# The order of 32-row and 64-row score products in a cross-attention kernel

## The chip, the cores and the metric

The kernel runs on one core of one Trainium2 chip. The metric is the device time of one execution in microseconds (us), the median of several runs. Five engines work from queues of their own: TensorE (PE in the profile, its weight loads PEld), VectorE (DVE), ScalarE (ACT), GpSimd (POOL) and SyncE (SP), which issues most of the DMAs. TensorE reads SBUF and writes PSUM; the results leave PSUM through VectorE and ScalarE.

## The reference

An image cross-attention layer on 16 items (the batch), float32, one after the other: 100 query rows of 640 numbers, 718 context rows of 384 numbers and 4 extra tokens of 384 numbers each. There are 8 heads of 80 numbers.

```python
query = hidden_states @ Wq            # (16, 100, 640)
keyt  = enc @ Wk                      # (16, 718, 640)
valt  = enc @ Wv
hs    = _mha(query, keyt, valt)       # softmax(q k^T / sqrt(80)) v, 8 heads
ca_q1 = einsum('btc,th->bch', ca, Wq_ca)[:, indices, :]   # 100 of 384 rows
ca_hs1 = _mha(ca_q1, residual, residual)                  # residual = hidden_states
ca_hs2 = _mha(ca_hs1 @ Wq, ca @ Wk_ca, ca @ Wv_ca)        # 4 tokens
out   = (hs + ca_hs2) @ Wout + b_out + residual
```

## The kernel before

**Stages.** One loop runs over the 16 items (`for b in range(B)`, called item 0 to item 15 here). Its order is written out by hand: the program stands in a manual schedule, so each engine executes its instructions in the order of the source. For item b the loop makes the scores of the 718 keys (`scores`, three groups), the larger of all scores per query (`larger`, then a `Maximum`, which spreads one maximum over 32-wide blocks: transposes and reductions on VectorE, two `spread` copies, on ScalarE where `scalar` is set), subtracts it, takes exponentials, and multiplies by the values (`a_ps`, line 1806). Beside that it makes the values of item b (`Values`, `vv`) and the keys of item b+1 (`Keys`, `kk`, and `Chunk` for the last 128 columns). Both use sums of the inputs' blocks to save products: `enc_sums` makes 13 such sums of 128x240 numbers on Pool for each item, of the context of item b+2, while item b runs.

The second attention (the 4 tokens, class `Second`) runs in small pieces between: `products` makes `y_ps` on TensorE out of `m2`, which `keys` fills on Pool from m's columns (`load_m` brings them from DRAM by a DMA on SyncE's queue); `copy` takes `y_ps` out (ScalarE to `y_sb`, line 968, and VectorE to `g`, line 964); `scores1` multiplies the tokens out on Pool (lines 980, 987); `softmax1` and `exponentials1` follow on VectorE and ScalarE; `softmax2` makes `z_ps` on TensorE; `scores2` subtracts a maximum (line 1062, on VectorE in item 1, on Pool in items after it); `values2` makes the result `hs2` on Pool from pieces `vb`, which SyncE loads, two ahead. `seen` is the last instruction of `larger(2)`; some loads and the first product of `scores1` are held back behind it.

Items are treated in three kinds: `MIXED` (3, 5, 7, 9, 11, 13), `PLAIN` (2, 4, 10, 12, 14) and the rest.

**Scores.** The 718 keys are cut into three thirds and each third into two halves of 120 or 119 keys; `KC` lists the six. A group g of `scores` covers two of them and fills four PSUM banks: bank r holds heads 2r and 2r+1. A head has 80 numbers; 64 of them stand in `qp`, two heads on top of each other in 128 partitions, the other 16 of each head stand in a common block `qz`, two heads in 32 rows. So there are 64-row products (`first_rows`: 64 partitions by 64 or 56 columns, four tiles of the array at once) and 32-row products (`last_rows`: 32 partitions by 120 columns, four at once). Each shows as two records in the profile (float32). A group has 64 records of the former and 16 of the latter.

```python
def first_rows(last):
    for a in range(2):
        u, j = KC[2 * g + a]
        for c in range(RG):        # 4 pairs of heads: c and 4 + c
            ...
...
steps = (last_rows, first_rows) if g == 1 else (first_rows, last_rows)
for i, step in enumerate(steps):
    step(i == 1)
```

Groups 0 and 2 take two pairs of banks (pool `ps2`), group 1 takes two banks of pool `psk` and two of pool `ps1`. The pools have two buffers of each kind. Just before item b's scores, `psk` holds the two banks of the last item's `a_ps` (head groups g = 0 and 1), and `ps1` holds that item's last key products and `y_ps`; `z_ps`, made behind the scores, is of `ps1` too. ScalarE copies the scores to SBUF (`st`): two copies of two banks each in groups 0 and 2 (line 837), four of one bank each in group 1 (line 831).

**The end of an item.** TensorE makes `a_ps` of head group 0, then of head group 1, with the steps of `Chunk` and of `softmax1` between them. `read(g)` divides by the sum of the exponentials and adds `hs2`: a reciprocal and four VectorE instructions (lines 1749, 1764). In PLAIN items both reads stand behind the last product; item 14 alone reads head group 0 earlier, with four ScalarE instructions and an addition on Pool (line 1773). Then come `products` and `copy` for item b+2's second attention, and item b+1's scores.

Of the kernel before, what the change touches and what calls it, by code (L numbers as in the profile page):

```python
# [14 lines left out]
B, S, H = 16, 100, 640  # L15
NH, D = 8, 80
CAD, T = 384, 4
SK = 722 - T
P = 128
HC = H // P  # L20
# [99 lines left out]
def kernel(  # L120
# [354 lines left out]
                at[:, : 2 * KT].rearrange("p (i k) -> p i k", i=2),  # L475
            )

    def enc_sums(enc):

        at = lambda f: a_form(enc, f)  # L480
        raw = lambda u, c: a_raw(enc, u - 1, c - 1)
        for out, left, right, op in (
            (at(7), raw(2, 3), raw(3, 1), ALU.add),
            (at(11), raw(3, 2), raw(3, 3), ALU.add),
            (at(8), at(11), raw(2, 3), ALU.subtract),
            (at(10), raw(1, 3), at(11), ALU.subtract),
            (at(9), raw(2, 1), raw(2, 2), ALU.add),
            (at(2), raw(1, 1), at(9), ALU.subtract),
            (at(9), at(9), raw(3, 1), ALU.subtract),
            (at(5), raw(1, 1), raw(2, 1), ALU.subtract),  # L490
            (at(5), at(5), raw(2, 3), ALU.add),
            (at(11), raw(1, 3), raw(3, 3), ALU.subtract),
            (at(11), at(11), raw(3, 1), ALU.add),
            (at(4), at(2), at(10), ALU.add),
            (at(4), at(4), raw(1, 2), ALU.add),
        ):
            nc.gpsimd.tensor_tensor(out, left, right, op)  # L497

    def w4(c, g):
# [266 lines left out]
    def scores(b, g, tiles):  # L766

        qp, qz = tiles
        name = f"s_ps_{b}_{g}"
        if g == 1:  # L770
            s_ps = [f(f"{name}_{r}") for r, f in enumerate((psumk, psumk, psum1, psum1))]
        else:
            pairs = [pair(f"{name}_{i}") for i in range(2)]
            s_ps = [pairs[r // 2][:, r % 2] for r in range(RG)]
        n = KN
        begun = set()

        def product(at, part, w, rhs, cols, last):

            k0, k1 = part  # L780
            nc.tensor.matmul(  # L781
                s_ps[at][k0:k1, cols],
                w,
                rhs,
                start=not begun & {(at, k) for k in range(k0, k1, 32)},
                stop=last,
                skip_group_check=True,
            )
            begun.update((at, k) for k in range(k0, k1, 32))

        def first_rows(last):

            for a in range(2):
                u, j = KC[2 * g + a]
                for c in range(RG):
                    rhs = qp[:, c // 2, c % 2, (b % 2) * S : (b % 2 + 1) * S]
                    for r in range(2):
                        h, rows = RG * r + c, slice(64 * r, 64 * r + 64)
                        lo = 256 * a + (h % 2) * S
                        for k0, k1 in KH:  # L800
                            product(
                                h // 2,
                                (k0, k1),
                                kT[rows, c, u, j * KN + k0 : j * KN + k1],
                                rhs[rows],
                                slice(lo, lo + S),
                                last,
                            )

        def last_rows(last):  # L810

            for a in range(2):
# [12 lines left out]
        steps = (last_rows, first_rows) if g == 1 else (first_rows, last_rows)  # L825
        for i, step in enumerate(steps):
            step(i == 1)
        st = sts[g][:n]
        if g == 1:
            for r in range(RG):  # L830
                nc.scalar.copy(  # L831
                    st[:, :, 2 * r * S : 2 * (r + 1) * S],
                    s_ps[r][:n].rearrange("p (a q) -> p a q", a=2)[:, :, : 2 * S],
                )
        else:
            for i in range(2):
                nc.scalar.copy(  # L837
                    st[:, :, 4 * i * S : 4 * (i + 1) * S].rearrange(
                        "p a (r q) -> p r a q", r=2
                    ),  # L840
                    pairs[i][:n].rearrange("p r (a q) -> p r a q", a=2)[:, :, :, : 2 * S],
                )
        return st

    def wait_for(ins, other):

# [632 lines left out]
            qmask, ident.rearrange("p (r u k) -> p u r k", r=RG, u=2), AX.XY, ALU.add  # L1479
        )  # L1480
    tiles = queries_tiles(0)
    for n in range(HC):
        queries(0, xT, tiles, n)

    xT_at = [None]
# [9 lines left out]
    for b in range(B):  # L1495
# [38 lines left out]
        if b == 0:  # L1534
            enc_sums(enc)
            now.load(nc.gpsimd)
        st.append(scores(b, 0, tiles))
        if b == 0:
            now.exponentials1()
        most = wide(f"most_{b}")  # L1540
        nc.vector.tensor_tensor(most, sts[0][:, 0], sts[0][:, 1], ALU.max)
        st.append(scores(b, 1, tiles))
        if b - 1 in PLAIN:
            now.exponentials1(2)
        larger(1)
        st.append(scores(b, 2, tiles))

        now.softmax2()
        if b == 0:
# [38 lines left out]
        elif b + 1 < B:  # L1588
# [14 lines left out]
                    nc.gpsimd.tensor_tensor(o, left, right, ALU.subtract)  # L1603
            elif last.b - 1 in PAIRS:
                nc.gpsimd.tensor_tensor(wout2[:, 0], wout2[:, 0], forms[0], ALU.add)
            second.scores1(seen, range(T - 1))
            top.go(3)
            kk.go(3)
            vv.go(3)
            now.scores2(nc.vector if b == 1 else nc.gpsimd)  # L1610
            second.scores1(None, range(T - 1, T))
            now.load(behind=seen)
            last.load(seen)
            top.go(1)
            if b > 1:
                last.place()
# [35 lines left out]
                nc.gpsimd.dma_start(out=bias, in_=bout[0].partition_broadcast(P))  # L1652
            if not mixed:
                second_next, enc_next = loads()
            if b + 2 < B:
                m_next = load_m(b + 2)
            late = mixed and last.b not in PAIRS
            if not late:
                subtract(2)
# [63 lines left out]
                )  # L1723
        if 0 < b < B - 2:
            keys(m_next)
            enc_sums(enc_next)
        held = b in MIXED and not second.less
        if b in MIXED and not held:
            second.exponentials1()
# [15 lines left out]
        def read(g):  # L1745
# [12 lines left out]
                return  # L1758
            for h in range(4):
                part = slice((4 * g + h) * D, (4 * g + h + 1) * D)  # L1760
                if b == B - 2 and g == 0:
                    nc.scalar.mul(hs[:S, part], a_v[:, h, :D], rs[:, h : h + 1])
                    continue
                nc.vector.scalar_tensor_tensor(
# [4 lines left out]
                    ALU.mult,  # L1769
                    ALU.add,  # L1770
                )
            if b == B - 2 and g == 0:
                nc.gpsimd.tensor_tensor(hs[:S, cols], hs[:S, cols], hs2[:, cols], ALU.add)

        if b in MIXED:
# [3 lines left out]
        for g in range(2):  # L1779
# [5 lines left out]
            for n, (h, i) in enumerate(order):  # L1785
                if b in PLAIN and (g, n) in ((1, 1), (1, 8), (1, 12)):
                    second.softmax1(1)
                    if b == B - 2 and n == 8:
                        read(0)
                if 0 < b < B - 1 and (g, n) in steps:  # L1790
                    chunk.go()
                    if b - 1 in PAIRS and b not in MIXED and (g, n) == (1, 6):
# [96 lines left out]
```

## Time and profile before

| | |
|---|---|
| median of 3 runs | 906.49 us (906.19 to 907.66) |
| the profiled execution | 907.72 us, span of its instructions 906.0 us |
| granted TensorE clock | 1.0 |
| TensorE busy | 900.3 us (99%), 12200 matmul records |
| VectorE, Pool, ScalarE busy | 720.6, 712.8, 461.9 us |

The profile is of one execution. A row of a timeline gives the start and the length in us, the engine, the line of the source, the operation, what is written and read (names without buffer numbers), the shape, and how many like instructions follow each other; in brackets stands how long the engine had been idle before, and who ended that. Matmuls overlap, so the cost of a run of them is read from its start to the start of the next run.

### The profile page before, as it was taken

To read this page: it belongs to the slowest core of one execution; us is meant where nothing else is said; L and a number is where in the kernel's file an instruction comes from. 1 tells how busy PE (TensorE), PEld (TensorE's weight loads), DVE (VectorE), ACT (ScalarE), POOL (GpSimd) and SP (SyncE) were. 2 spreads that over 40 slices of the span, in tenths; PEclk is the share of its full clock that TensorE was granted. 3 is DMA by queue.
4 is the path that set the end of the run, shared out by engine and by line. 5 is a ranking of instruction groups with operands and counts; after the bars stand their busy time and mean duration, and the time that the engine had idled before them with its cause. 6 is when DMAs were issued, how large, how long until landed. Compare 5 with 4: busy or idle time off the path is not lost.

```text
span 906.0 us, 28486 instructions
## 1 busy us (share of the span) xinstructions
PE 900.3 (99%) x12200; PEld 748.1 (83%) x12200; DVE 720.6 (80%) x1278; ACT 461.9 (51%) x917; POOL 712.8 (79%) x684
## 2 busy tenths in 40 slices
PE   9999999999999999999999999999999999999998
PEld 6898889787797878878798787988879788797866
DVE  3669796999849898786987869788984899848893
ACT  2344543747437564644737446375742747437451
POOL 8689998787868889696896959958897688976633
PEclk9999999999999999999999999999999999999999
DMA  8723111132301212230122301203130031310111
GB/s 292 264 70 92 36 58 43 37 95 53 112 4 52 80 41 67 54 105 32 53 56 53 106 34 52 56 25 107 54 83 32 24 107 53 98 32 24 62 47 38
DMA packets 50627, 63.00 MB, mean 70 GB/s; under 512 B 13594, under 2 KB 37850, under 8 KB 50500
## 3 DMA queue, kind: packets, MB, share of 16 engines
q1 hardware_dynamic: 48852, 59.18, 21.4%
q8 instruction: 96, 1.57, 0.7%
q10 hardware_dynamic: 1024, 1.15, 0.4%
q0 software_dynamic: 624, 0.85, 0.3%
q14 instruction: 31, 0.25, 0.1%
HBM read 55.59 MB, written 5.57 MB: 68 GB/s over the span
## 4 chain that ended last, share of the span: by engine, by line
PE 94%; DVE 5%; ACT 0%; DMA 0%; issue 0%; DVEq 0%
PE a_ps L1806 12%; PE s_ps L781 12%; PE v_psA L431 10%; PE k_psA L462 8%; PE v_psB L431 8%; PE k_psB L462 6%; PE o_ps L1259 5%; PE k_psA L742 4%; PE v_psC L431 3%; PE k_psC L462 3%; PE v_ps L372 2%; PE q_ps L599 2%; PE q_ps L541 2%; PE v_psD L431 2%; PE v_psE L431 2%; PE k_psE L462 1%
## 5 line engine op out<-in xcount | busy, mean ns | idle before, releaser
L980 POOL TENSOR_TENSOR e<-ca,g 100x800 f32<-100x800 f32 x64 | 97.9, 1540 | 90.9 <-ACT kT L404 67.4
L1806 PEld LDWEIGHTS a_ps<-vs,st 120*64 120x64 f32 (+3 forms) x3072 | 119.0, 124 | 10.1 <-issue 0.7
L497 POOL TENSOR_TENSOR enc<-enc 128x240 f32<-128x240 f32 x144 | 113.2, 796 | 14.2 <-DMA enc<-in_enct 7.2
L1806 PE MATMUL a_ps<-vs,st 120*64 120x81 f32 (+3 forms) x3072 | 122.8, 233 | 0.0
L1517 DVE TENSOR_TENSOR st<-st,over 120x1600 f32<-120x1600 f32 x48 | 116.6, 2431 | 0.0
L431 PE MATMUL v_psA<-wv_sb,enc 128*120 128x320 f32 x352 | 109.3, 433 | 0.0
L1098 POOL TENSOR_TENSOR hs<-hs,hs 100x640 f32<-100x640 f32 x48 | 94.8, 1975 | 3.8
L987 POOL TENSOR_TENSOR e<-e,e 100x800 f32<-100x800 f32 x48 | 93.4, 1945 | 3.8
L462 PE MATMUL k_psA<-enc,wk_sb 128*128 128x240 f32 x384 | 95.2, 371 | 0.2 <-DVE kT L402 0.2
L1091 POOL TENSOR_TENSOR hs<-vb,p 100x640 f32<-100x640 f32 x64 | 90.6, 1426 | 3.8 <-DMA vb<-va_d 1.5
L431 PE MATMUL v_psB<-wv_sb,enc 128*120 128x320 f32 x296 | 91.9, 433 | 0.0
L1525 ACT ACTIVATE st<-st 120x1600 f32<-120x1600 f32 x48 | 73.9, 1539 | 23.5 <-DVE st L1517 23.2
L462 PEld LDWEIGHTS k_psA<-enc,wk_sb 128*128 128x128 f32 x384 | 71.5, 190 | 16.4 <-issue 1.2
L431 PEld LDWEIGHTS v_psA<-wv_sb,enc 128*120 128x120 f32 x352 | 64.2, 183 | 25.0 <-DVE vs L402 0.5
L1529 DVE TENSOR_TENSOR most<-most,st 120x800 f32<-120x800 f32 x64 | 68.0, 1063 | 14.3 <-ACT st L831 13.2
L462 PE MATMUL k_psB<-enc,wk_sb 128*128 128x240 f32 x320 | 77.9, 366 | 0.0
L781 PE MATMUL s_ps<-qp,kT 64*56 64x100 f32 (+1 forms) x3072 | 73.3, 248 | 0.0
L431 PEld LDWEIGHTS v_psB<-wv_sb,enc 128*120 128x120 f32 x296 | 54.1, 183 | 21.8 <-DVE vs L402 0.4
L781 PEld LDWEIGHTS s_ps<-qp,kT 64*56 64x56 f32 (+1 forms) x3072 | 67.0, 130 | 5.5 <-issue 4.2
L837 ACT COPY st<-s_ps 120x800 f32<-120x800 f32 x64 | 49.8, 830 | 38.7 <-PE s_ps L781 38.5
L1166 ACT COPY hsT<-turned_hs 32x160 f32<-32x160 f32 (+7 forms) x244 | 67.7, 278 | 3.0
L462 PEld LDWEIGHTS k_psB<-enc,wk_sb 128*128 128x128 f32 x320 | 60.9, 190 | 7.9
(213 smaller groups left out, 1905.9 us busy)
## 6 DMA issues: line engine op xcount, KB each, us to landing
vb<-va_d SPq DMA_DIRECT2D x62, 250.0 KB
enc<-in_enct SPq DMA_DIRECT2D x30, 240.0 KB
enc<-in_enct SPq DMA_DIRECT2D x15, 360.0 KB
xT<-in_xt SPq DMA_DIRECT2D x8, 500.0 KB
rest<-in_enct SPq DMA_DIRECT2D x31, 120.0 KB
xn<-in_x SPq DMA_DIRECT2D x11, 320.0 KB
out<-xn SPq DMA_DIRECT2D x11, 320.0 KB
ca<-in_cas SPq DMA_DIRECT2D x16, 156.2 KB
```

The costliest lines, as they stand in the source:

```text
L431: nc.tensor.matmul(at[0][j][:KN, : H // 2], a_form(self.enc, f)[:, j * KN : (j + 1) * KN], wv_there.get(f, wv_sb[:, W_AT[f]]), start=first ...
L462: nc.tensor.matmul(at[:, i * KT : (i + 1) * KT], wk_sb[:, W_AT[f], i], a_form(self.enc, f), start=(first and i == 0), stop=last, skip_grou ...
L497: nc.gpsimd.tensor_tensor(out, left, right, op)
L781: nc.tensor.matmul(s_ps[at][k0:k1, cols], w, rhs, start=not begun & {(at, k) for k in range(k0, k1, 32)}, stop=last, skip_group_check=True,)
L980: first = nc.gpsimd.tensor_tensor(to, self.ca[:, t, :].unsqueeze(1).to_broadcast([S, NH, S]), g[:, :, t].unsqueeze(2).to_broadcast([S, NH, ...
L987: made = nc.gpsimd.tensor_tensor(e, e, to, ALU.add)
L1091: first = nc.gpsimd.tensor_tensor(to, self.vb[t][:S].rearrange("p (h d) -> p h d", h=NH), p2[:, :, t].unsqueeze(2).to_broadcast([S, NH, D] ...
L1098: nc.gpsimd.tensor_tensor(sums, sums, to, ALU.add)
L1517: return nc.vector.tensor_tensor(st[i], st[i], top.over[:KN].unsqueeze(1).to_broadcast([KN, 2, ROWS]), ALU.subtract,)
L1525: nc.scalar.activation(st[i], st[i], AF.Exp, scale=SCALE)
L1529: most_now = nc.vector.tensor_tensor(most[:KN], most[:KN], st[i][:, u], ALU.max)
L1806: nc.tensor.matmul(a_v[lo:hi, h % 4], st[i // 2][: KEYS[i], i % 2, h * S + lo : h * S + hi], block(i, h // 4)[: KEYS[i], h % 4], start=(i ...
```

## The change

It makes the following edits:

- `scores` becomes a generator. For items 0 to 14 groups 0 and 1 first make their 32-row products, one group after the other; then group 0 makes its 64-row products and is copied, then group 1. Group 2 keeps its order (64-row, then 32-row). Item 15 keeps the old order in all groups.
- In `first_rows` the loop over c is now outside the one over a, so banks 0 and 2 are complete after the first half of the products, banks 1 and 3 after the second.
- Groups 0 and 1 are copied by four ScalarE copies of one bank each, in the order 0, 2, 1, 3.
- The queries of item 0 begin with the last column block, which holds the 16-number rests.
- `load_m` of item b+2 stands right behind the loads that wait for `seen`, ahead of `values2`, no longer behind item b+2's other loads.
- In item 1 `scores2` subtracts on Pool, and `scores1` stands behind it as a whole.
- In items 2, 4, 10 and 12 `read(0)` stands among head group 1's products (behind the third), with ScalarE's four instructions and Pool's addition as in item 14; five of the 13 `enc_sums` come before it, eight after.

The diff, cut to its core:

```diff
-    def enc_sums(enc):
+    def enc_sums(enc, lo=0, hi=None):
...
-        ):
+        )[lo:hi]:
             nc.gpsimd.tensor_tensor(out, left, right, op)
...
-            for a in range(2):
-                u, j = KC[2 * g + a]
-                for c in range(RG):
+            for c in range(RG):
+                for a in range(2):
+                    u, j = KC[2 * g + a]
...
-        steps = (last_rows, first_rows) if g == 1 else (first_rows, last_rows)
-        for i, step in enumerate(steps):
-            step(i == 1)
...
+            if g < 2:
+                for r in (0, 2, 1, 3):
+                    nc.scalar.copy(
+                        st[:, :, 2 * r * S : 2 * (r + 1) * S],
+                        s_ps[r][:n].rearrange("p (a q) -> p a q", a=2)[:, :, : 2 * S],
+                    )
...
+        if g == 0 and b == B - 1:
+            first_rows(False)
+            last_rows(True)
+            yield
+        elif g < 2:
+            last_rows(False)
+            yield
+            first_rows(True)
         else:
...
+            first_rows(False)
+            last_rows(True)
+        yield copies()
...
-    for n in range(HC):
+    for n in (HC - 1, *range(HC - 1)):
         queries(0, xT, tiles, n)
...
-        st.append(scores(b, 0, tiles))
+        parts = [scores(b, g, tiles) for g in range(2)]
+        for part in parts:
+            next(part)
+        st.append(next(parts[0]))
...
-        st.append(scores(b, 1, tiles))
+        st.append(next(parts[1]))
...
-        st.append(scores(b, 2, tiles))
+        st.extend(scores(b, 2, tiles))
...
-            second.scores1(seen, range(T - 1))
+            if b > 1:
+                second.scores1(seen, range(T - 1))
...
-            now.scores2(nc.vector if b == 1 else nc.gpsimd)
-            second.scores1(None, range(T - 1, T))
+            now.scores2(nc.gpsimd)
+            if b > 1:
+                second.scores1(None, range(T - 1, T))
+            else:
+                second.scores1()
             now.load(behind=seen)
             last.load(seen)
+            if b + 2 < B:
+                m_next = load_m(b + 2)
...
-            if b + 2 < B:
-                m_next = load_m(b + 2)
...
             keys(m_next)
-            enc_sums(enc_next)
+            enc_sums(enc_next, 0, 5 if b in PLAIN else None)
...
-                if b == B - 2 and g == 0:
+                if b in PLAIN and g == 0:
                     nc.scalar.mul(hs[:S, part], a_v[:, h, :D], rs[:, h : h + 1])
...
-            if b == B - 2 and g == 0:
+            if b in PLAIN and g == 0:
                 nc.gpsimd.tensor_tensor(hs[:S, cols], hs[:S, cols], hs2[:, cols], ALU.add)
...
-                    if b == B - 2 and n == 8:
-                        read(0)
+                if b in PLAIN and (g, n) == (1, 8 if b == B - 2 else 3):
+                    read(0)
+                    if b < B - 2:
+                        enc_sums(enc_next, 5)
...
-            for g in (1,) if b == B - 2 else range(2) if b in PLAIN else (g,):
-                read(g)
+            read(g)
```

More of the change, by code (lines that the diff above doesn't have):

```diff
@@ L823, in last_rows, with copies @@
                     )
-        steps = (last_rows, first_rows) if g == 1 else (first_rows, last_rows)
-        for i, step in enumerate(steps):
-            step(i == 1)
[L828 to L834, printed above, removed]
-        else:
[L836 to L843, printed above, removed]
+        def copies():
+            st = sts[g][:n]
+            if g < 2:
[5 more added lines that the diff above has]
+            else:
+                for i in range(2):
+                    nc.scalar.copy(
+                        st[:, :, 4 * i * S : 4 * (i + 1) * S].rearrange(
+                            "p a (r q) -> p r a q", r=2
+                        ),
+                        pairs[i][:n].rearrange("p r (a q) -> p r a q", a=2)[
+                            :, :, :, : 2 * S
+                        ],
+                    )
+            return st
+        if g == 0 and b == B - 1:
[6 more added lines that the diff above has]
+            first_rows(True)
+        else:
+            first_rows(False)
+            last_rows(True)
+        yield copies()
     def wait_for(ins, other):
@@ L1609 @@
             vv.go(3)
-            now.scores2(nc.vector if b == 1 else nc.gpsimd)
-            second.scores1(None, range(T - 1, T))
+            now.scores2(nc.gpsimd)
+            if b > 1:
+                second.scores1(None, range(T - 1, T))
+            else:
+                second.scores1()
             now.load(behind=seen)
             last.load(seen)
+            if b + 2 < B:
+                m_next = load_m(b + 2)
             top.go(1)
```

## The prediction

> **What bounds the kernel now.** I read the page's first part, then TensorE's timeline through the score blocks, then the other engines' timelines beside it, and last the places where TensorE stands idle.
>
> ```profile
> span 906.0 us, 28486 instructions
> ```
> ```profile
> PE 900.3 (99%) x12200; PEld 748.1 (83%) x12200; DVE 720.6 (80%) x1278; ACT 461.9 (51%) x917; POOL 712.8 (79%) x684
> ```
>
> TensorE is the bound: 900.3 of 906.0 us. Another engine's time counts only where TensorE waits for it. So there are two questions: what the new order saves on TensorE itself, and which waits appear or go. TensorE's timeline of one score block (item 3; columns: start, length, engine, line, operation, tile, count) shows the first.
>
> ```profile
> 198.25 1.60 PE L781 MATMUL s_ps<-qp,kT 64*64 64x100 f32 x64
> 199.78 1.63 PE L781 MATMUL s_ps<-qz,kT 32*120 32x200 f32 x32
> 201.34 2.97 PE L781 MATMUL s_ps<-qp,kT 64*64 64x100 f32 x128
> 204.24 0.95 PE L781 MATMUL s_ps<-qz,kT 32*120 32x200 f32 x16
> 205.12 0.75 PE L1021 MATMUL z_ps<-y_sb,e 100*32 100x33 f32 x64
> ```
>
> No row has a wait in brackets. From start to start, 64 records of 64-row products take 1.53 us and 128 take 2.90, so 64 further ones take 1.37 and opening a run of them costs 1.53 - 1.37 = 0.16. For 32-row products 16 records take 0.88 and 32 take 1.56: 16 further ones 0.68, opening a run 0.20. A change of the row height costs TensorE 0.16 to 0.20 us, and one block makes four runs.
>
> **The switch removed.** The new order (32-row products of thirds 0 and 1, then all 64-row ones, then the 32-row ones of the last third) makes three runs: 1.56 + (2.90 + 1.37) + 0.88 = 6.71 us, where the rows have 1.53 + 1.56 + 2.90 + 0.88 = 6.87. That is 0.16; other blocks round to 0.13, and I take 0.15. The block now begins with 32-row products behind the 128-row products of `y_ps`. No row shows that entry; bounds are the two opening costs (0.16 and 0.20), so it could take back 0.04, or, if a run's opening is mostly a matter of what stands ahead of it, nothing; I take nothing. Item 15 keeps the old order, so 15 blocks x 0.15 = 2.25 us less.
>
> **The waits added.** The four banks of group 1 used to be needed 1.5 us after the block's start plus most of a 32-row run. Now group 1's first products come right behind group 0's 16 records: between 0.68 and 0.88 us after the start, so about 0.79. Two of these banks held `a_ps` (freed by the reads of `read`), the last one held `y_ps`, freed by ScalarE's copy of y and then VectorE's copy g. Everything behind the fourth product waits in TensorE's queue. An ordinary boundary (into item 8), with the price of a wake-up:
>
> ```profile
> 475.30 1.60 PE L781 MATMUL s_ps<-qp,kT 64*64 64x100 f32 x64
> ```
> ```profile
> 475.41 0.37 ACT L968 COPY y_sb<-y_ps 100x256 f32<-100x256 f32 x1 [2.32 <-PE y_ps L951]
> ```
> ```profile
> 474.88 0.93 DVE L1764 SCALAR_TENSOR_TENSOR hs_sb<-a_ps,rs,hs 100x80 f32<-100x80 f32 x4
> 475.81 0.19 DVE L964 COPY g<-y_ps 100x32 f32<-100x32 f32 x1
> ```
> ```profile
> 773.55 0.48 DVE L402 TENSOR_TENSOR vs<-v_psC,vs 120x320 f32<-120x320 f32 x1
> ```
> ```profile
> 772.77 0.97 PE L462 MATMUL k_psB<-enc,wk_sb 128*128 128x240 f32 x4
> 774.08 1.08 PE L462 MATMUL k_psC<-enc,wk_sb 128*128 128x240 f32 x4 [0.34 <-DVE vs L402]
> ```
>
> The last three rows: VectorE ends at 774.03, TensorE goes on at 774.08 (0.05 later), and its first four records take 1.08 instead of 0.97, so a wake-up costs 0.05 and about 0.1 for weights that could not be loaded ahead. Into item 8, g ends at 476.00, 0.70 after the block's start; 0.70 + 0.15 = 0.85 against 0.79: 0.06 lost. Nine boundaries look like this (into items 2, 4, 6, 7, 8, 9, 10, 12, 14): 0.5 us, with 0 and 0.1 each as bounds.
>
> Into items 3, 5, 11 and 13, which follow the items of PLAIN, ScalarE is busy:
>
> ```profile
> 197.14 1.73 ACT L899 COPY spread<-mx 64x800 f32<-64x800 f32 x2
> 198.89 0.37 ACT L968 COPY y_sb<-y_ps 100x256 f32<-100x256 f32 x1
> ```
> ```profile
> 198.81 0.93 DVE L1764 SCALAR_TENSOR_TENSOR hs_sb<-a_ps,rs,hs 100x80 f32<-100x80 f32 x4
> 199.65 0.18 DVE L964 COPY g<-y_ps 100x32 f32<-100x32 f32 x1
> ```
>
> The moved read of head group 0 takes the first of VectorE's two sets of four reads (0.93 each) away, so its second set ends as in the ordinary boundary. But y's copy stays behind the two `spread` copies, which the change leaves where they are: it ends at 199.26, g then at 199.26 + 0.03 + 0.19 = 199.48, TensorE is back at 199.63 against 198.25 + 0.79 = 199.04. Lost 0.59, four times: 2.4 us (bounds 0.45, without the wake-up's refill, and 0.65). Without the moved read it would be 199.83 for g, 0.35 more each time; that is all this edit is worth, and its ScalarE reads and the Pool add behind them (0.86 us a piece at item 14) lie beside head group 1's products, with no reader on TensorE.
>
> Into item 1:
>
> ```profile
> 94.87 1.60 PE L781 MATMUL s_ps<-qp,kT 64*64 64x100 f32 x64
> ```
> ```profile
> 95.03 0.88 ACT L1014 ACTIVATE e<-e 100x800 f32<-100x800 f32 x1 [5.86 <-DVE rs L1749]
> 95.81 0.35 ACT L968 COPY y_sb<-y_ps 100x256 f32<-100x256 f32 x1
> ```
> ```profile
> 96.19 0.19 DVE L964 COPY g<-y_ps 100x32 f32<-100x32 f32 x1 [0.64 <-ACT y_sb L968]
> ```
>
> g starts only when y's copy has ended (96.16, then 96.19) and ends at 96.38; 96.53 against 95.66: 0.87 lost (0.4 if the exponential came half a microsecond earlier). Into item 0 the banks held `q_ps`; queries of the last column block now come first, and the other copies (0.33 us each) end within 0.5 of the start: nothing lost. Score blocks together: -2.25 + 0.5 + 2.4 + 0.87 = +1.5 us.
>
> **Four copies for two.**
>
> ```profile
> 200.82 1.56 ACT L837 COPY st<-s_ps 120x800 f32<-120x800 f32 x2 [1.56 <-PE s_ps L781]
> 202.69 1.68 ACT L831 COPY st<-s_ps 120x400 f32<-120x400 f32 x4 [0.31 <-PE s_ps L781]
> ```
>
> Four take 1.68 where two take 1.56. Group 2's first products need all four copies of group 0. With two banks complete halfway (0.69 into group 0's 1.37) and the 0.31 from product to copy seen here, they run from 1.00 to 2.68 after group 0's 64-row start; TensorE reaches group 2 at 2 x 1.37 + 0.05 = 2.79, and 2.68 + 0.05 is before that. Nothing, with 0 and 0.15 a block as bounds: the margin is 0.06.
>
> **The waits removed.** In item 1 VectorE subtracts `mx` from `s2`:
>
> ```profile
> 110.83 1.28 DVE L1062 TENSOR_TENSOR e<-s,mx 100x32 f32<-100x32 f32 x1
> ```
> ```profile
> 282.02 0.24 POOL L1062 TENSOR_TENSOR e<-s,mx 100x32 f32<-100x32 f32 x1
> ```
> ```profile
> 111.14 0.97 PE L462 MATMUL k_psB<-enc,wk_sb 128*128 128x240 f32 x4
> 111.95 1.24 PE L431 MATMUL v_psE<-wv_sb,enc 128*120 128x320 f32 x4
> 113.03 1.24 PE L431 MATMUL v_psA<-wv_sb,enc 128*120 128x320 f32 x4
> 114.48 1.05 PE L462 MATMUL k_psA<-enc,wk_sb 128*128 128x240 f32 x4 [0.20 <-DVE kT L402]
> 115.55 1.08 PE L462 MATMUL k_psE<-enc,wk_sb 128*128 128x240 f32 x4
> 116.46 0.97 PE L431 MATMUL v_psB<-wv_sb,enc 128*120 128x320 f32 x3
> ```
>
> It takes 1.28 us beside Pool's products, 0.24 on Pool in other items; TensorE's steps of 0.81 and 1.08 become 1.45, 1.07 and 0.91, 0.73 late in all. On Pool, with the token products behind it, VectorE is 1.2 us ahead there and the 0.73 goes. The token products of that item now stand behind it, and their end, 124.14, may come a little later; VectorE reads them 9 us after that:
>
> ```profile
> 120.78 3.36 POOL L987 TENSOR_TENSOR e<-e,e 100x800 f32<-100x800 f32 x1
> ```
> ```profile
> 133.24 1.00 DVE L872 STREAM_TRANSPOSE turned<-e 128x800 f32<-128x800 f32 x1
> ```
>
> In item 13 TensorE waits 774.08 - 772.77 - 0.81 = 0.50 and refills for 0.1, in item 11 0.28 and 0.1: 0.98 us. VectorE's queue is late there:
>
> ```profile
> 769.29 4.33 DVE L1517 TENSOR_TENSOR st<-st,over 120x1600 f32<-120x1600 f32 x1
> ```
> ```profile
> 740.56 1.40 POOL L922 TENSOR_TENSOR m<-mb,hmask 128x64 f32<-128x64 f32 x5 [3.31 <-DMA mb<-m_d]
> ```
> ```profile
> 751.06 2.91 DVE L1529 TENSOR_TENSOR most<-most,st 120x800 f32<-120x800 f32 x2 [0.55 <-ACT st L831]
> ```
> ```profile
> 204.40 2.02 DVE L1529 TENSOR_TENSOR most<-most,st 120x800 f32<-120x800 f32 x2 [0.55 <-ACT st L831]
> ```
>
> Pool waits 3.31 us for m's columns, so its sums run into the next item and slow VectorE's maxima (2.91 against 2.02 in item 3); 0.9 us later everything on VectorE, the subtraction that fell on Pool's adds included. With the columns asked for ahead of vb's second pieces the 3.31 goes, and Pool's new add (0.86) takes back a quarter: item 13 should look like item 3, which has no such wait. -0.98, bounds 0 and -0.98. The Trainium skill, "SBUF — State Buffer", section "Who interferes with whom", has a VectorE instruction with two SBUF inputs fully blocked by a Pool instruction that reads SBUF; by that the long maxima and the 4.33 are one cause, which the rows bear out.
>
> **Sum.** -2.25 + 0.5 + 2.4 + 0.87 - 0.73 - 0.98 = -0.2 us of the profiled execution's 907.72 (span 906.0). The median of the runs is 906.49, so 906.3. I call 0.2% (1.8 us) what a measurement can tell from no change.
>
> **Rivals.** *Emptying costs more, waking less* (faster): if a removed change of height is worth the 0.20 of a 32-row opening, and the refill of 0.1 after a wait is covered by the three products ahead of it, 15 x 0.05 + 14 x 0.1 = 2.15 less: 904.2. The 0.20 is in the rows; for the refill they speak against it. Chance 0.25.
>
> *The copies come too late* (slower): group 2 waits for the fourth copy in every block. It decides from 0.06 us on; a delay of 0.06 beyond that and a refill of 0.1 make 0.16 x 15 = 2.4: 908.7. For it the thin margin, against it that ScalarE is idle 1.56 us before the copies. The Trainium skill, "TensorEngine Tiling (Array Packing)", section "PSUM Bottleneck", warns that emptying PSUM may become the bottleneck of a tiled array. The rows show the price (1.68 against 1.56), not yet a wait. Chance 0.12.
>
> *The collision moves* (slower): Pool's later add and later token products meet VectorE's subtraction elsewhere. The 0.98 stays and 0.6 comes twice: 908.5. Chance 0.10.
>
> *The switch is not saved* (the change doesn't do what it says): entering 32-row products from `y_ps` costs as much as the removed run. +2.25: 908.6. Chance 0.08.
>
> **How the numbers follow.** The forecast has 0.45, of which 0.42 falls within 0.2%. Faster by over 0.2%: 0.25, nearly all from the first rival. Slower: 0.27, from the other three. The rest, 0.48, is within. The range 904.1 to 908.8 takes in the prices of all the rivals at their given size and leaves about 0.15 outside.
>
> **What would show it.** Right: three runs in each score block, blocks 0.1 us shorter at nine boundaries, gaps of 0.6 us inside the 32-row run of items 3, 5, 11, 13 and 0.9 in item 1, released by g; no waits at `k_psA` of item 1 and `k_psC` of items 11 and 13. Wrong: no gap in items 3, 5, 11 and 13; a wait of group 2's first product for ScalarE; a subtraction of over 4 us at a new place.

## The result, and the profile after

| | before | after |
|---|---|---|
| median of 4 runs each, same chip | 906.38 us | 916.31 us (915.99 to 916.59) |
| ratio, 95% interval | | 1.011 (1.0098 to 1.0123) |
| span of the profiled execution | 906.0 us | 914.9 us |
| granted TensorE clock | 1.0 | 1.0 |

The change is 9.9 us slower. The forecast was 906.3 us with a range up to 908.8: ten microseconds too low.

TensorE's timeline of the score block of item 8 after the change (start, length, engine, line, operation, tile, shape, count), and the first product behind it:

```profile
480.81 1.71 PE L781 MATMUL s_ps<-qz,kT 32*120 32x200 f32 x32
482.45 5.01 PE L781 MATMUL s_ps<-qp,kT 64*64 64x100 f32 x192
487.39 0.95 PE L781 MATMUL s_ps<-qz,kT 32*120 32x200 f32 x16
488.27 0.75 PE L1035 MATMUL z_ps<-y_sb,e 100*32 100x33 f32 x64
```

There are three runs, as the edit intends. But the run of 192 records takes 487.39 - 482.45 = 4.94 us from start to start, where the rows of before give 2.90 + 1.37 = 4.27: 0.67 too long. The row has no wait in brackets, because the modelled lengths of the products ahead cover a gap of this size. TensorE's weight loads show it in the same stretch; their brackets give the idle time and what ended it:

```profile
482.45 2.78 PEld L781 LDWEIGHTS s_ps<-qp,kT 64*64 64x64 f32 x128 [0.24 <-issue]
485.48 0.19 PEld L781 LDWEIGHTS s_ps<-qp,kT 64*64 64x64 f32 x4 [0.25 <-ACT st L830]
485.87 1.39 PEld L781 LDWEIGHTS s_ps<-qp,kT 64*64 64x64 f32 x60 [0.21 <-ACT st L830]
```

The first 128 loads belong to groups 0 and 1. Group 2 then waits twice for ScalarE's copies, at its first products into each pair of banks. ScalarE's four copies of group 0 in the same block:

```profile
484.14 1.68 ACT L830 COPY st<-s_ps 120x400 f32<-120x400 f32 x4 [2.84 <-PE s_ps L781]
```

They start 484.14 - 482.45 = 1.69 after the 64-row start and end at 3.37; the prediction had 1.00 and 2.68. Over the whole execution (the view of waits):

```profile
PEld s_ps L781 <- ACT st L830: 6.9, 30, 0.3
```

That is 30 waits, two in each of 15 blocks; with the refill of weights behind each wait it comes to 0.67 x 15 = 10.0 us.

Where the 8.9 us of span lie, from TensorE's records: from the last product ahead of the scores (of `y_ps` in most items) to the first of `z_ps` the 16 blocks take 124.16 us where they took 112.77, that is 11.38 more. Between the blocks item 1 is 0.73 shorter, item 11 0.38, item 13 0.61, and a gap of 0.18 in item 6's `z_ps` is gone. The stretch behind the last product, in which the last output leaves by DMA, is 0.64 shorter. It is 3.41 to 3.45 us in the nine traces here that have all the small edits, and 3.79 to 4.43 in the four that lack some of them; which edit does it was not tried.

### The profile page after: what moved, and what is told of

Read it like the earlier page. It is cut to its first block, busy times and chain, and to the rows that moved or that the text cites. A ratio compares the mean times of both kernels' runs of the same rounds, so it can differ in the third digit from the quotient of the medians.

```text
span 914.9 us, 28533 instructions
## 1 busy us (share of the span) xinstructions
PE 908.8 (99%) x12200; PEld 752.4 (82%) x12200; DVE 714.8 (78%) x1261; ACT 466.1 (51%) x965; POOL 710.1 (78%) x689
## 3 DMA queue, kind: packets, MB, share of 16 engines
q8 instruction: 96, 1.57, 0.7%
## 4 chain that ended last, share of the span: by engine, by line
PE 95%; ACT 2%; DVE 2%; issue 0%; DMA 0%; ACTq 0%; DVEq 0%
PE a_ps L1829 11%; PE s_ps L781 11%; PE v_psA L431 11%; PE v_psB L431 9%; PE k_psA L462 9%; PE k_psB L462 7%; PE o_ps L1273 5%; PE k_psA L742 4%; PE v_psC L431 4%; PE k_psC L462 3%; PE v_ps L372 2%; PE q_ps L599 2%; ACT st L830 2%; PE q_ps L541 2%; PE v_psD L431 2%; PE v_psE L431 2%
## 5 line engine op out<-in xcount | busy, mean ns | idle before, releaser
L497 POOL TENSOR_TENSOR enc<-enc 128x240 f32<-128x240 f32 x144 | 107.2, 754 | 12.8 <-DMA enc<-in_enct 6.0
L1112 POOL TENSOR_TENSOR hs<-hs,hs 100x640 f32<-100x640 f32 x48 | 96.2, 2005 | 3.8
L781 PE MATMUL s_ps<-qp,kT 64*56 64x100 f32 (+1 forms) x3072 | 78.8, 249 | 1.1
L781 PEld LDWEIGHTS s_ps<-qp,kT 64*56 64x56 f32 (+1 forms) x3072 | 69.5, 130 | 11.0 <-ACT st L830 6.9
L830 ACT COPY st<-s_ps 120x400 f32<-120x400 f32 x128 | 52.4, 530 | 43.1 <-PE s_ps L781 43.1
L1543 DVE TENSOR_TENSOR most<-most,st 120x800 f32<-120x800 f32 x64 | 65.8, 1028 | 10.5 <-ACT st L830 9.4
```

Of the source, the lines that this page charges most:

```text
L781: nc.tensor.matmul(s_ps[at][k0:k1, cols], w, rhs, start=not begun & {(at, k) for k in range(k0, k1, 32)}, stop=last, skip_group_check=True,)
L830: nc.scalar.copy(st[:, :, 2 * r * S : 2 * (r + 1) * S], s_ps[r][:n].rearrange("p (a q) -> p a q", a=2)[:, :, : 2 * S],)
L1112: nc.gpsimd.tensor_tensor(sums, sums, to, ALU.add)
```

## The experiments

Theory A says that the copies are late because they start late: the program tracks PSUM by tile, so a copy waits for every product into its tile, and the two banks of a pair of groups 0 and 2 are one tile. Its rivals: ScalarE cannot copy fast enough wherever it starts (B), or the long run is long by itself (C).

**The banks dealt the other way.** In the changed kernel tile 0 holds banks 0 and 1, one of which is written to the very end. Here tile 0 holds banks 0 and 2, both complete halfway.

```diff
-            s_ps = [pairs[r // 2][:, r % 2] for r in range(RG)]
+            s_ps = [pairs[r % 2][:, r // 2] for r in range(RG)]
...
-                        st[:, :, 4 * i * S : 4 * (i + 1) * S].rearrange(
-                            "p a (r q) -> p r a q", r=2
-                        ),
+                        st.rearrange("p a (r i q) -> p i r a q", r=2, i=2)[:, i],
```

> The changed kernel (916.3 us), with the banks of groups 0 and 2 dealt to the two-bank tiles the other way: tile 0 holds banks 0 and 2, tile 1 holds banks 1 and 3. Nothing else moves; the four single-bank copies keep their order 0, 2, 1, 3. Theory A, the tile: in the changed kernel the copy of bank 0 waits for the last product into its two-bank tile, and that is the last product of the whole group, so the copies start 1.69 us after the 64-row start (482.449 to 484.142 in item 8) where the prediction had 1.00. Here tile 0 is complete halfway, copies start near 1.00 and end near 2.7, group 2's first product at 2.79 finds tile 0 long free. The 0.67 us that each of 15 blocks loses goes: 916.3 - 10.0 = 906.3 us (906 to 907). Theory B, ScalarE's capacity: four copies in 1.37 us of products cannot keep up wherever they start, or reading a tile whose other bank is being written slows them: copies end after 2.79 again, 911 to 916 us. Theory C, the run of 192 products is longer for a reason of its own (the row's waits are a symptom): 916.

Measured: 909.61 us (8 runs), 1.0029 of before (1.0018 to 1.0039; before on this chip, and in the next three runs, is 906.64). Item 8, TensorE, then ScalarE:

```profile
480.07 4.34 PE L781 MATMUL s_ps<-qp,kT 64*64 64x100 f32 x192
484.35 0.95 PE L781 MATMUL s_ps<-qz,kT 32*120 32x200 f32 x16
```
```profile
481.11 1.68 ACT L830 COPY st<-s_ps 120x400 f32<-120x400 f32 x4 [2.18 <-PE s_ps L781]
```

The copies start 1.04 after the 64-row start and end at 2.72, and the run takes 4.28 from start to start. In no block does TensorE wait for a copy of the scores. Theory A holds, B and C fall: the same four copies, started 0.65 earlier, cost nothing. The time fell by 6.7 us, though, not by 10. In item 1 g is later (y's copy stands behind an exponential, and this waits for a slow subtraction on VectorE): 0.75. The rest lies in gaps that no engine releases, here in item 9:

```profile
534.84 1.70 PE L781 MATMUL s_ps<-qz,kT 32*120 32x200 f32 x32
536.47 3.49 PE L781 MATMUL s_ps<-qp,kT 64*64 64x100 f32 x151
540.41 1.10 PE L781 MATMUL s_ps<-qp,kT 64*56 64x100 f32 x41 [0.46 <-issue]
```

"issue" means that the engine waited for nothing that the profile shows. Such gaps stand in the scores of seven items and in the `z_ps` products of another, 4.0 us in all (each product's spacing beyond that of the same product in the other items). What they are is taken up below.

**Half of group 0's copies on VectorE.**

```diff
-                for r in (0, 2, 1, 3):
-                    nc.scalar.copy(
+                for r in (0, 2, 1, 3) if g else range(RG):
+                    copy = nc.vector.tensor_copy if g == 0 and r > 1 else nc.scalar.copy
+                    copy(
```

> The changed kernel, with group 0's copies shared: ScalarE copies banks 0 and 1, VectorE banks 2 and 3; all still start only when the group's products have ended (1.69 us after the 64-row start). Theory A: two copies in a row end at 1.69 + 0.385 + 0.50 = 2.58, before group 2 at 2.79, so most of the 0.67 a block goes; in items 3, 5, 11, 13 VectorE is busy until 204.18 in item 3, 0.3 us behind the start of the copies, and would still hold TensorE for about 0.2. 906.3 to 908 us. Theory B (capacity of ScalarE): the same, 906 to 908. Theory C: 916. This one tells C from the other two and gives the price of the copies on VectorE.

Measured: 911.66 us, 1.0056 (1.0044 to 1.0068). Item 8, VectorE and TensorE:

```profile
481.04 1.05 DVE L831 COPY st<-s_ps 120x400 f32<-120x400 f32 x2 [1.86 <-PE s_ps L781]
```
```profile
479.34 4.48 PE L781 MATMUL s_ps<-qp,kT 64*64 64x100 f32 x192
483.75 0.95 PE L781 MATMUL s_ps<-qz,kT 32*120 32x200 f32 x16
```

The copies still start at 1.70, VectorE's two end at 2.75, and 4.41 remains of the 4.94, 0.14 over the free run. In items 3, 5, 11 and 13 VectorE is late and up to 0.4 more is lost. The expected 908 was too low by the 0.14 in each block, by item 15 (0.6, where VectorE is late too) and by 1.9 us of the gaps above. It is against C all the same: half the copies' time, and most of the wait is gone. The Trainium skill, "TensorEngine Tiling (Array Packing)", section "PSUM Bottleneck", advises emptying PSUM with both engines. Here that took 4.7 us off, and dealing the banks so that a tile is complete early took 6.7.

**Two copies of two banks for group 0.**

```diff
-            if g < 2:
+            if g == 1:
                 for r in (0, 2, 1, 3):
```

> The changed kernel, with group 0 copied as in the kernel before: two copies of a two-bank tile each instead of four of one bank. Theory A: both start where the four do, 1.69 after the 64-row start; tile 0 is free at 1.69 + 0.83 = 2.52, before group 2 at 2.79, tile 1 at 1.69 + 1.56 + 0.05 = 3.30, so TensorE loses 0.50 + 0.05 = 0.55 a block where the changed kernel loses 0.67: 916.3 - 15 x 0.12 = 914.5 us. Theory B (the number of copies is what costs): back to no wait, 906 to 908. If copying each bank alone does help: slower than 916.3.

Measured: 914.98 us, 1.0088 (1.0075 to 1.0101). Item 8, ScalarE and TensorE:

```profile
482.74 1.55 ACT L836 COPY st<-s_ps 120x800 f32<-120x800 f32 x2 [2.83 <-PE s_ps L781]
```
```profile
481.05 3.13 PE L781 MATMUL s_ps<-qp,kT 64*64 64x100 f32 x132
484.34 1.58 PE L781 MATMUL s_ps<-qp,kT 64*64 64x100 f32 x60 [0.17 <-ACT st L836]
```

Both start at 1.69 as well, the first pair is released before it is needed (132 records run through), the second costs 0.54. So copying each bank alone brought nothing in the changed kernel and cost 0.13 a block. Whether it pays with tiles that are complete halfway was not run.

**The old scores with all other edits** (`scores` and its calls as in the kernel before).

> The changed kernel with the scores of the kernel before (four runs, two-bank copies of groups 0 and 2, the old order of columns); every other edit stays: m's columns early, the products of item 1 on Pool, token products behind it, head group 0 read on ScalarE and Pool, queries of the last column block first. By the prediction's terms this leaves -0.73 (item 1) and -0.98 (items 11 and 13): 906.4 - 1.7 = 904.7 us (904.3 to 905.2). If these waits only moved to another place, 906.4; if the new reads and Pool's additions hold something up, over 906.6.

Measured: 905.28 us (11 runs), 0.9981 (0.9973 to 0.999): the one version that is faster than both kernels by more than the interval. Beside the trace of before the blocks are as long (item 11's is 0.22 shorter); between the blocks item 1 is 0.73 shorter, item 11 0.37, item 13 0.60, and so is the stretch behind the last product, by 0.64. At the place of item 11's old wait TensorE's steps are the full 0.81:

```profile
661.97 0.97 PE L462 MATMUL k_psB<-enc,wk_sb 128*128 128x240 f32 x4
662.78 0.97 PE L462 MATMUL k_psC<-enc,wk_sb 128*128 128x240 f32 x4
663.59 1.24 PE L431 MATMUL v_psA<-wv_sb,enc 128*120 128x320 f32 x4
```

**The new scores alone, in the kernel before.**

> The kernel before (906.5 us) with nothing but the new scores and their order of calls. By the prediction's terms the other edits are worth -1.7 here and, in items 3, 5, 11 and 13, 0.35 each for the read that is not moved; so this is slower than the changed kernel by 1.7 + 1.4: 916.3 + 3.1 = 919.4 us (918 to 920). If the moved read is worth nothing: 918.0. If the other edits only pay together with the new order: under 917.

Measured: 920.74 us, 1.0154 (1.0138 to 1.0169), beside 907.10 for before on that chip. Item 3:

```profile
201.13 1.27 PE L781 MATMUL s_ps<-qz,kT 32*120 32x200 f32 x18
202.76 0.95 PE L781 MATMUL s_ps<-qz,kT 32*120 32x200 f32 x14 [0.35 <-DVE g L978]
203.63 5.01 PE L781 MATMUL s_ps<-qp,kT 64*64 64x100 f32 x192
```

The block of this item is 0.35 longer than in the changed kernel, and so are those of items 5, 11 and 13 (0.35 to 0.36): the price put on the moved read. Item 0 waits for the copy of the last column block's queries (0.8 for `qz` in the view of waits), which their new order avoids; the expected 919.4 did not have this. The waits at `k_psC` of items 11 and 13 do not come back, though m's columns are late again (Pool waits up to 2.97 us for them) and VectorE's maxima have their short times. The last run below returns to this.

**y's copy ahead of the spread copies, and in item 0 ahead of the exponential.**

```diff
-                        if b in PLAIN:
+                        if b == B - 2:
                             second.softmax1(1)
-                        else:
+                        elif b not in PLAIN:
...
-                second.exponentials1()
...
         if b + 2 < B:
             second_next.products()
             second_next.copy()
+        if b == 0:
+            second.exponentials1()
```

> The changed kernel (916.3 us), with ScalarE's copy of y ahead of the two spread copies in items of PLAIN but the last, and ahead of the exponential in item 0; the banks' copies stay late. Expected by the prediction's terms for the added waits, as the trace shows them: the 32-row run of items 3, 5, 11 and 13 falls from 1.89 to the ordinary 1.37 us (-0.52 each), that of item 1 from 2.14 to about 1.5 (-0.6): 916.3 - 2.7 = 913.6 us. If y's copy does not set these waits (VectorE's reads do): 916.3. If the later spread copies hold up the exponentials ahead of z's products: between the two or slower.

Measured: 914.06 us, 1.0076 (1.0062 to 1.009), beside 907.10. Item 3:

```profile
199.66 1.74 PE L781 MATMUL s_ps<-qz,kT 32*120 32x200 f32 x32
201.33 5.01 PE L781 MATMUL s_ps<-qp,kT 64*64 64x100 f32 x192
```

The 32-row run takes 1.67 to the next start instead of 2.14 in the changed kernel (200.02 to 202.16), item 1's block is 0.54 shorter. So y's copy did set these waits.

**What the gaps of "issue" are.** The page's DMA part and a window around item 9's gap in the kernel with the banks dealt the other way:

```profile
q8 instruction: 96, 1.57, 0.7%
```
```profile
GB/s 0 0 0 0 0 0 0 0 0 0 0 94 0 0 0 0 0 0 0 0 0 0 0 0 0 0 0 0 0 0 0 0 94 0 0 0 0 0 0 0
```

96 packets bring 1.57 MB, 16384 bytes each. TensorE's program holds 6115 products. All but 30 are four instructions each (two records, each with a weight load); the 30 transposes show one record and one load. With some others, for semaphores, the trace has 24,623 records, or 96.2 times 256. So one packet is 256 instructions. In the second row, 536 to 543 us in 40 slices, two packets come in the 12th and the 33rd slice, 3.6 us apart. Counted with four instructions for every product, as in the expectations below, the gaps of items 3, 5, 9 and 12 stand at 231 to 234 past a multiple of 256, those of items 0 and 1 at 223. That count takes two too many for each transpose, of which 15 stand ahead of item 0 and 5 between items 1 and 2. Counted by the trace's own records, all these gaps stand at 192 to 194. This is theory F: TensorE has run out of instructions and the refill is late. In the long run 256 instructions last 2.73 us (4 per 2 x 21.3 ns). Shift the count, and the gaps must move:

```diff
-    for _ in range(21):
+    for _ in range(21 + 32):
         nc.tensor.matmul(
             idle_ps[:32, :32], idle[:, :32], idle[:, :32], start=True, stop=True
         )
```

> The kernel with the banks dealt the other way (909.6 us), with 32 more idle products of 32 x 32 ahead of all work, where TensorE waits for the first weights anyway. They only move every later instruction of TensorE by 128 places. With the copies out of the way seven blocks (items 0, 1, 3, 5, 9, 12, 14) kept gaps of up to 0.7 us that no engine releases. Counted in TensorE's own instructions (four to a product of float32), the gaps of items 3, 5, 9 and 12 all lie at 231 to 234 past a multiple of 256, those of items 0 and 1 at 223, and the instruction transfers in the trace are 16384 bytes each, some 96 for some 24,700 instructions: one per 256. Theory F, the refill: TensorE has used up its instructions, and the next 256 are not there. Then the gaps move with the count: none in items 3, 5, 9, 12 (their second boundary falls out of the long run), instead gaps at the same remainder in items 2, 4, 6, 8, 10 as far as their refills are late; 906.0 to 909.5 us. Rival: the gaps belong to the items (an engine or a transfer of that item): the same items and the same products as before, 909.6.

Measured: 915.14 us, 1.0095 (1.008 to 1.0111), beside 907.10. Item 9, with the gap before the shift, and item 8, without one:

```profile
538.33 4.35 PE L781 MATMUL s_ps<-qp,kT 64*64 64x100 f32 x192
542.61 0.95 PE L781 MATMUL s_ps<-qz,kT 32*120 32x200 f32 x16
```
```profile
481.13 3.65 PE L781 MATMUL s_ps<-qp,kT 64*64 64x100 f32 x157
485.21 1.07 PE L781 MATMUL s_ps<-qp,kT 64*64 64x100 f32 x35 [0.43 <-issue]
486.21 0.95 PE L781 MATMUL s_ps<-qz,kT 32*120 32x200 f32 x16
```

The gaps have left the scores of items 0, 1, 3, 5, 9 and 12 and come in items 2, 6 and 8, in the `z_ps` products of seven items and in item 4's key products; the small one of item 14 stands 64 records, or 128 instructions, earlier. Each of 0.2 us or more stands at 193 or 194 by the trace's records. Here that of item 5:

```profile
319.50 0.47 PE L1033 MATMUL z_ps<-y_sb,e 100*32 100x33 f32 x33
320.43 0.45 PE L1033 MATMUL z_ps<-y_sb,e 100*32 100x33 f32 x31 [0.46 <-issue]
```

Nothing but the count of instructions was changed ahead of them, so theory F holds. The packets themselves bear it out: in this run, in that with the banks dealt the other way and in the two shifted ones that follow, every gap of 0.2 us or more ends 1.2 to 1.6 us after the last packet has ended. For item 9's gap the packet ran from 538.03 to 538.96, and the products go on at 540.41. The price was mis-sized: I looked for late refills in the scores alone, and the boundary after next, in `z_ps`, is late too. 6.2 us are lost in the scores and `z_ps`, not the 4 at most that the expected range allows. And the shift may not be free, as I had taken it to be: 106 idle records now last until 6.9 us, and the last product of `q_ps` ahead of item 0's scores starts at 57.3 us. Without the shift it starts at 55.6 to 56.3 in all traces but that of the old scores with all other edits, which has 57.9, so scatter may be part of it.

```profile
1.13 5.82 PE L1345 MATMUL idle_ps<-idle 128*32 128x32 f32 x106 [1.13 <-DVE idle L1342]
```

**All three together** (banks dealt the other way, y early, the shift):

> All three together: banks dealt the other way, y's copy early, 32 more idle products at the start. If no instruction were late, every one of 15 blocks would take 6.94 us where the kernel with the old scores has 7.03: 905.3 - 15 x 0.085 = 904.0 us. Theory F adds late refills in items 2, 4, 6, 8, 10, up to 0.7 each and about half of that on the mean: 905.7 us (904 to 907.5). Without theory F: 904.0.

Measured: 913.39 us, 1.0074 (1.0061 to 1.0087), beside 907.10. Several blocks now take the 6.94 us, and the view of waits shows what took the gain:

```profile
PE z_ps L1033 <- issue: 5.0, 8, 1.0
```

With the gaps inside the scores 8.5 us are lost at the boundaries. The faster the products run up to them, the longer TensorE waits for its instructions.

**The shift under the old scores.** Is the old order free of this bound?

> The kernel with the old scores and all other edits (905.3 us), with the same 32 idle products at the start. In the two kernels without the wait for copies the late refills went with the count of instructions (all at 223 to 234 past a multiple of 256). The old order's block needs 7.03 us for the 480 instructions of the scores, hardly more than the 6.94 of the new one, so it should lie near the same bound: with the boundaries 128 places on, they fall into z's products in items 0, 1, 3, 5, 12 and 14 (about 2.9 us after the boundary ahead, where refills took up to 3.4), and up to 0.5 is lost in each: 906 to 908 us, gaps at the same remainder. If the refill bound belongs to the run of 192 products alone: no gaps, 905.3.

Measured: 907.43 us (11 runs), 1.0013 (1.0004 to 1.0022), where the same kernel without the shift had 905.28. Item 11:

```profile
641.32 0.55 PE L1021 MATMUL z_ps<-y_sb,e 100*32 100x33 f32 x38
642.07 0.41 PE L1021 MATMUL z_ps<-y_sb,e 100*4 100x33 f32 x26 [0.20 <-issue]
```

Six such gaps, some 1.8 us, all at 193 or 194 by the trace's records, in `z_ps` of items 0, 3, 11, 12, 13 and 15; the trace without the shift has none of them. The trace of the kernel before has one: item 6's 0.18, at 193 and 1.48 us after a packet. By time alone it is less plain: the idle products may cost something at the start too, and this trace, of the slowest execution of the 11, also has 0.5 in item 11's `o_ps` products, most of it a wait for Pool. So the old order runs just under the same bound. How much of it shows depends on where the boundaries fall.

**The two small edits, each alone in the kernel before.** m's columns early:

> The kernel before (906.5 us) with one edit alone: m's columns are asked for early. By the prediction: Pool's wait of 3.31 us for them goes, its sums end earlier, VectorE's maxima of item 13 fall from 2.91 to about 2.0, the subtraction of 4.33 to under 3.8, and TensorE's waits at k_psC in items 11 and 13 go: -0.98 us, 905.5. If something else on Pool sets VectorE's delay: both waits stay, 906.5.

Measured: 905.97 us, 0.9996 (0.9987 to 1.0005): inconclusive by time. In the trace Pool's multiplication of m starts without the 3.31 of wait, VectorE's maxima and subtraction are short, and TensorE's waits at `k_psC` are gone. Pool, then VectorE, item 13 and the stretch before it:

```profile
733.42 3.02 POOL L1098 TENSOR_TENSOR hs<-hs,hs 100x640 f32<-100x640 f32 x1
736.40 1.40 POOL L922 TENSOR_TENSOR m<-mb,hmask 128x64 f32<-128x64 f32 x5
```
```profile
750.25 2.02 DVE L1529 TENSOR_TENSOR most<-most,st 120x800 f32<-120x800 f32 x2 [0.70 <-ACT st L831]
768.25 3.68 DVE L1517 TENSOR_TENSOR st<-st,over 120x1600 f32<-120x1600 f32 x1
```

Item 1's subtraction on Pool:

> The kernel before (906.5 us) with one edit alone: in item 1 the products and the subtraction of scores2 run on Pool, with the token products behind them. By the prediction VectorE gains 1.2 us there and TensorE's wait at k_psA goes: -0.73 us, 905.8. If the token products, now later, hold up VectorE's transposes of e in item 1: 906.5 or more.

Measured: 906.0 us, 0.9997 (0.9988 to 1.0006), again inconclusive by time; in the trace the steps at `k_psA` are full ones:

```profile
112.93 1.24 PE L431 MATMUL v_psA<-wv_sb,enc 128*120 128x320 f32 x4
114.00 0.97 PE L462 MATMUL k_psA<-enc,wk_sb 128*128 128x240 f32 x4
114.81 0.97 PE L462 MATMUL k_psE<-enc,wk_sb 128*128 128x240 f32 x4
```

This edit acts in item 1 alone, and m's columns are asked for late as before. Yet here, too, VectorE's subtraction in item 13 is short and TensorE's waits at `k_psC` are gone:

```profile
737.38 1.41 POOL L922 TENSOR_TENSOR m<-mb,hmask 128x64 f32<-128x64 f32 x5 [1.62 <-DMA mb<-m_d]
```
```profile
767.57 3.69 DVE L1517 TENSOR_TENSOR st<-st,over 120x1600 f32<-120x1600 f32 x1
```
```profile
772.09 0.97 PE L462 MATMUL k_psC<-enc,wk_sb 128*128 128x240 f32 x4
772.90 1.24 PE L431 MATMUL v_psA<-wv_sb,enc 128*120 128x320 f32 x4
```

Pool waits 1.62 for the columns, not 3.31, and nothing behind it is late. So the waits at `k_psC` are not in every execution that asks late. The trace of before is of an execution of 907.72 us, 1.2 above the median; less the 0.98 of these waits and the 0.22 of item 11's block it would be 906.5. That the early columns take 0.98 off the median is not shown.

Only the run with all the small edits together clears what the measurement can tell.

## Why the prediction was wrong

- **Four copies for two** is the step that failed. It took the banks to be released one by one, "with two banks complete halfway", and so had the copies run from 1.00 to 2.68. They run from 1.69 to 3.37, because the copy of bank 0 waits for the last product into its two-bank tile, which is the last of the group. Priced at nothing with 0.15 as a bound, it costs 0.67 a block, 10.0 us in all. The run with the banks dealt the other way gives the 1.04 to 2.72 that the step had reckoned: its arithmetic was right for a program in which a bank is a tile. The error was to read the order of the products and not what the copies wait for. A wait of group 2 for ScalarE is one of the prediction's own signs of being wrong.
- The rival **The copies come too late** had the mechanism (group 2 waits for the fourth copy) and the right point of decision, but let the copies be late by 0.06. Its 908.7 was 7.6 us short.
- **The switch removed** and the ordinary boundaries were right: without the wait for copies (the banks dealt the other way) the block of item 8 takes 6.94 us instead of 7.03, which is -0.15 and +0.07, where I had -0.15 and +0.06. The entry behind `y_ps` took nothing back.
- **The waits added**: items 3, 5, 11 and 13 show a 32-row run of 1.89 us, from its first start to its last, against 1.30 without a wait, which is 0.59 as worked out; item 1 has 0.84 against the 0.87 forecast. The two runs on y's copy and on the moved read bear out both causes.
- **The waits removed**: -0.73 in item 1 as forecast, -0.98 in items 11 and 13 together (0.38 and 0.61), from trace to trace. But the sum set a term read from an execution of 907.72 us against the median of 906.49. The run with item 1's subtraction on Pool lacks the 0.98 though its columns are late, so this term may be nothing in the median; the forecast would then have been 907.3. Item 13 after the change, where the rows of before had 2.91 and 4.33:

```profile
760.41 2.02 DVE L1543 TENSOR_TENSOR most<-most,st 120x800 f32<-120x800 f32 x2 [0.59 <-ACT st L830]
778.52 3.63 DVE L1531 TENSOR_TENSOR st<-st,over 120x1600 f32<-120x1600 f32 x1
```

- So, from trace to trace, all terms but one came out within 0.1 us a block. The sum was wrong by that one; the doubt about the 0.98 is a tenth of it.
- What none of the cases had: the saved switch did not pay in any run. Where the copies are out of the way, TensorE meets the refill of its instructions. The wait for the copies hides this: in the changed kernel no late refill shows in these blocks.

## What to carry to other kernels

Work out when a buffer comes free from the unit in which the program tracks it, not from the last write to the part that is read: a copy of one bank waits for every product into a tile of two. Where products end in an order, deal the banks so that the ones that end together share a tile. And before packing a stage of small products more tightly, divide its time by its instructions: where 256 of them go by faster than the 3.3 us that two packets were apart here at least, a gap with no releaser, always at the same remainder of the instruction count, says that TensorE is waiting for its program. Last, see whether a wait that you mean to remove is in an ordinary execution, or only in the one that was traced.

## What the runs showed of the hardware

- TensorE's instructions arrive in packets of 16384 bytes, one per 256 instructions. The late refills cost up to 0.80 us in a score block and 1.16 us in `z_ps`, with the packets 3.3 to 3.7 us apart where TensorE ran fastest.
- Not every fast stretch is late: in the kernel with the banks dealt the other way the 256 instructions across the boundaries took 2.68 to 2.75 us in items 7, 11 and 13 without a gap, and 3.46 and 3.48 with one in items 9 and 5. In the first three the packet started 0.25 to 0.43 us after the boundary ahead (the place 193 past a multiple of 256), in the eight places with a gap 0.56 to 1.19. What makes a packet start later stays open; the gap of item 9 has no other transfer beside it (the row of slices above).
- A copy of 120x400 from PSUM takes 0.56 us on VectorE (the mean of 32) and 0.52 on ScalarE (of 96).
